# Rows asked for by need, and the opening of a state-space and attention kernel put together anew

## The chip, the cores and the metric

The kernel runs on one core of a Trainium2 chip. The metric is the device time of one execution in microseconds. All data are fp32 apart from two small mask tables in bf16.

## The reference

Two layers, for 8 images of 384 channels and 32 x 32 pixels (1024 tokens). Cut to what matters:

```python
# layer 0, per batch element: a state-space recurrence in both directions, beside a local convolution
xn = x * rsqrt(mean(x*x over channels) + 1e-6) * norm_w
u, z = split(in_proj_w @ xn)                      # 384 channels each
for each direction:                               # tokens forward, tokens backward
    uc    = silu(causal 4-tap depthwise conv of u + conv1d_b)
    dt, Bm, Cm = split(x_proj_w @ uc)             # 24, 16 and 16 rows
    delta = softplus(dt_proj_w @ dt + dt_proj_b)
    h[n]  = exp(delta * A[n]) * h[n] + (delta * uc) * Bm[n]     # 16 states for each channel, along 1024 tokens
    y     = (sum over n of h[n] * Cm[n] + uc * D_param) * silu(z)
g  = out_proj_w @ (y forward + y backward) * scale_mod
lf = sigmoid(3x3 depthwise conv of xn + dw_b) * xn
x  = x + res_scale * (g + lf)
# layer 1, on tokens: causal attention with 6 heads, then a feed-forward block
t  = t + attention(layernorm(t))
t  = t + ffn(layernorm(t))    # sign-binarized weights, activations scaled by their maximum over a group
```

The groups of the feed-forward block's scaling are single batch elements here, and only five of them get anything from it (the reference leaves the rest at zero).

## The kernel before, in words

Channels lie on the 128 partitions in NC = 3 chunks, tokens along the free dimension in two halves of 512. The work consists of three kinds of pieces. Each piece is a list of steps with an estimated time, and the steps of pieces that run together are put in one order by these times. A scheduler then fixes each engine's order: instructions have the priority of the order in which they were emitted, and one that is ready earlier may move ahead. Each engine, and each DMA queue, keeps its order.

`before_scan(b, ...)` (L305) makes what the recurrence of batch b needs. It loads xn, normalizes it, and for each chunk projects it (`in_proj`, L333: four PSUM banks, each of three matmuls, copied out by ACT), runs the 4-tap convolution for two directions and two halves (`conv`, L345: the first tap by ACT, L352, the other three by DVE into PSUM, L362; ACT adds the bias, L363), runs the 3x3 convolution (`local`, L367: nine taps, eight of them on DVE, L383), applies silu and tanh and the residual (`gates`, L417, with a change of ACT's function table before and after), and projects u to the rows of dt, B and C (`project`, L450). Results go to DRAM ("spill"): u in both directions, their sum, silu(z), and the residual with the local part. After the three chunks the rows of B and C are written to DRAM, and twelve `delta` steps (L477) compute delta and delta*u, with four ACT and four DVE instructions each, and store both (L497).

The recurrence is cut in 768 units: a batch, a chunk, one of four parts (direction and half), and two of the 16 states. For a unit the rows of B and of C are read from DRAM and spread over 128 partitions by DMA (tiles bc0 and bc1, 512 KB each). POOL multiplies delta*u by B's rows (L539), ACT computes the decay exp(delta*A) (L552), DVE scans (L557, one scan for each of the two states, in place in the tile g), POOL multiplies by C's rows (L563), and PE adds up over states by transposing g into a PSUM bank (L573). What is done for which unit in slot k stands in `slots` (L1032): the loads of unit k+3, POOL's first product of unit k+2, scans and second product of unit k, the sum of unit k-1. POOL's own order is kept as written. The tile g has 7 buffers, bc0 has 3 and bc1 has 4; they share the SBUF with a pool of 12 `mid` tiles of 1024 elements and 6 `big` tiles of 3072.

`attention` and `feed_forward` of batch b (L621, L905) follow the recurrence of batch b. The first batch's `before_scan` runs alone. Beside the 96 units of its recurrence stand, in this order, the second batch's `before_scan`, `binarize` for w1 and w2 (L194), and the `before_scan` of the third and fourth batch (L1060 to L1066). All later units run beside attention, feed-forward and the other batches' `before_scan` (L1068 to L1090); the last batch's attention comes alone at the end (L1091).

Nearly all loads and stores go through SP's queue (`load`, L109; `spill`, L121; the stores at L254, L472, L497 and L617). SP issues them in its order and stands still at the first one whose tile is not yet free or whose data is not yet made.

Of the kernel before, what the change touches and what calls it, by code (L numbers as in the profile page):

```python
# [9 lines left out]
F32 = mybir.dt.float32  # L10
# [42 lines left out]
def kernel(  # L53
# [19 lines left out]
    const = ctx.enter_context(tc.tile_pool(name="const", bufs=1))  # L73
    small = ctx.enter_context(tc.tile_pool(name="small", bufs=4))
    big = ctx.enter_context(tc.tile_pool(name="big", bufs=6))
    mid = ctx.enter_context(tc.tile_pool(name="mid", bufs=12))
    ptp = ctx.enter_context(tc.tile_pool(name="ptp", bufs=2))
    sp = ctx.enter_context(tc.tile_pool(name="scan", bufs=2))
    dram = ctx.enter_context(tc.tile_pool(name="dram", bufs=5, space=DRAM))
# [114 lines left out]
    def binarize(src, dst, nk, nout, per, name, emit):  # L194

        gs = nout // GROUPS
        st = {}

        def part(w, k, n):
            return w[k * P : (k + n) * P, :].rearrange("(k p) e -> p k e", p=P)  # L200

        def view(k, n):
            t = btile(f"{name}_{k}")
            v = t.rearrange("p c l -> p (c l)")[:, : n * nout].rearrange("p (k e) -> p k e", k=n)
            load(v, part(src, k, n))
            return v

        starts = list(range(0, nk, per))

        @emit  # L210
        def _():
            st["ones"] = small.tile([P, P], F32, name=f"ones_{name}", tag="bones", bufs=1)
            nc.vector.memset(st["ones"], 1.0 / (gs * nk * P))
            st["mps"] = bank(f"mps_{name}", "av")

        for k in starts:

# [15 lines left out]

        @emit
        def _():
            st["mean"] = small.tile([P, GROUPS], F32, name=f"mean_{name}", tag="bmean", bufs=1)
            nc.vector.tensor_copy(st["mean"], st["mps"][:, :GROUPS])

        for k in starts:

            @emit
            def _(k=k, n=min(per, nk - k)):
                v = view(k, n)
                for g in range(GROUPS):
                    z = v[:, :, g * gs : (g + 1) * gs]
                    nc.vector.tensor_scalar(z, z, st["mean"][:, g : g + 1], None, ALU.subtract)
                t = btile(f"sg_{name}_{k}")
                sg = t.rearrange("p c l -> p (c l)")[:, : n * nout].rearrange("p (k e) -> p k e", k=n)
                z, sg = v[:, :, : GROUPS * gs], sg[:, :, : GROUPS * gs]
                nc.scalar.activation(sg, z, AF.Sign)  # L250
                nc.vector.tensor_tensor(sg, sg, z, ALU.subtract)
                nc.vector.tensor_tensor(z, z, sg, ALU.add)
                nc.vector.memset(v[:, :, GROUPS * gs :], 0.0)
                nc.sync.dma_start(out=part(dst, k, n), in_=v)  # L254


    def mean_of(c_of, name):
# [44 lines left out]
                    )  # L302


    def before_scan(b, tags, emit):  # L305

        st = {}
        turns = itertools.cycle(tags)
# [36 lines left out]
        def conv(c, d, h):  # L345

            acc = bank_of(f"u{d}_{b}_{c}_{h}")
            up = st["up", c]
            for s in range(DCONV):
                w = vec[:, c, V_CW + DCONV - 1 - s : V_CW + DCONV - s]  # L350
                if s == 0:
                    nc.scalar.activation(acc, up[:, half(h)], AF.Copy, scale=w)  # L352
                    continue
                lo, hi = h * HB, (h + 1) * HB
                if d == 0:
                    t0, t1 = max(lo, s), hi
                    tap = up[:, t0 - s : t1 - s]
                else:
                    t0, t1 = lo, min(hi, L - s)
                    tap = up[:, t0 + s : t1 + s]  # L360
                to = acc[:, t0 - lo : t1 - lo]
                nc.vector.scalar_tensor_tensor(to, tap, w, to, ALU.mult, ALU.add)  # L362
            nc.scalar.activation(  # L363
                st["u", d, c][:, half(h)], acc, AF.Identity, bias=vec[:, c, V_CB : V_CB + 1]
            )

        def local(c, h):  # L367

            acc = bank_of(f"loc_{b}_{c}_{h}")
            r0, rows = h * (HB // W), HB // W  # L370
            img = acc.rearrange("p (i j) -> p i j", j=W)
            src = st["xn"][:, c, :].rearrange("p (i j) -> p i j", j=W)
            nc.scalar.activation(  # L373
                acc, st["xn"][:, c, half(h)], AF.Copy, scale=vec[:, c, V_DW + 4 : V_DW + 5]
            )
            for k in range(9):
                di, dj = k // 3 - 1, k % 3 - 1
                if k == 4:
                    continue
                i0, i1 = max(r0, -di), min(r0 + rows, H - di)  # L380
                j0, j1 = max(0, -dj), W - max(0, dj)
                to = img[:, i0 - r0 : i1 - r0, j0:j1]
                nc.vector.scalar_tensor_tensor(  # L383
                    to,
                    src[:, i0 + di : i1 + di, j0 + dj : j1 + dj],
                    vec[:, c, V_DW + k : V_DW + k + 1],
                    to,
                    ALU.mult,
                    ALU.add,
                )  # L390
            return acc

        for c in range(NC):

            @emit
            def _(c=c):
                w = mtile(f"win_{b}_{c}", NC * 2 * P).rearrange("p (k i e) -> p k i e", k=NC, i=2)
                for i in range(2):
                    load(
                        w[:, :, i, :],  # L400
                        w_in[:, i * C + c * P : i * C + (c + 1) * P].rearrange("(k p) e -> p k e", p=P),
                    )
                st["win", c] = w
                st["up", c] = mtile(f"up_{b}_{c}")
                st["z", c] = mtile(f"z_{b}_{c}")
                for d in range(2):
                    st["u", d, c] = mtile(f"u{d}_{b}_{c}")

            for i in range(2):
                for h in range(NH):  # L410
                    emit(lambda c=c, i=i, h=h: in_proj(c, i, h), 2.6)
            for d in range(2):
                for h in range(NH):
                    emit(lambda c=c, d=d, h=h: conv(c, d, h), 3.0)


            def gates(c=c):  # L417
                st["xc"] = mtile(f"xc_{b}_{c}")
                load(st["xc"], x[b, chunk(c), :])
                accs = [local(c, h) for h in range(NH)]  # L420
                with tc.high_priority(offset=60):
                    for t in (st["u", 0, c], st["u", 1, c], st["z", c]):
                        pin(nc.scalar.activation(t, t, AF.Silu))
                    for h in range(NH):
                        pin(
                            nc.scalar.activation(
# [12 lines left out]
                usum = mtile(f"us_{b}_{c}")  # L439
                nc.vector.tensor_tensor(usum, st["u", 0, c], st["u", 1, c], ALU.add)  # L440
                spill((b, "us", c), usum, f"sus_{b}_{c}")
                for d in range(2):
                    spill((b, "u", d, c), st["u", d, c], f"su_{d}_{b}_{c}")

            emit(gates, 14.0)


            for h in range(NH):
# [75 lines left out]
    def s_load(u):  # L524
        if u.n == 0:
            for what in ("ud", "dl"):
                t = sp.tile([P, HB], F32, name=f"{what}_{u.name}", tag=what)
                load(t, spilled[u.b, what, u.d, u.c, u.h])
                sst[what, u.b, u.c, u.part] = t
        for i in range(2):  # L530
            r = sp.tile([P, 2, HB], F32, name=f"bc{i}_{u.name}", tag=f"bc{i}", bufs=3 + i)
            rows = spilled[u.b, "rows", u.d][i * NS + u.n : i * NS + u.n + 2, half(u.h)]
            load(r, rows.partition_broadcast(P))
            sst["bc", i, u.name] = r

    def s_first(u):
        g = sp.tile([P, 2, HB], F32, name=f"g_{u.name}", tag="g", bufs=7)
# [494 lines left out]
    def slots(lo, hi):  # L1032
# [2 lines left out]
                f(units[k])  # L1035

        def slot(k):
            at(s_load, k + AHEAD + 1)
            at(s_first, k + AHEAD)
            at(s_scan, k)  # L1040
            at(s_sum, k - 1)
            at(s_gate, k - 1)
# [4 lines left out]
        for f, _ in spread_over(*lists):  # L1047
            f()

    def steps_of(stage, *args):  # L1050
        out = Steps()
        stage(*args, out)
        return out

    per, ahead = len(units) // B, 3
    first = slots(-AHEAD - 1, per + 1)
    others = slots(per + 1, len(units) + 1)
    run(steps_of(before_scan, ORDER[0], ("s", "pt")))  # L1060
    beside = steps_of(before_scan, ORDER[1], ("s", "pt"))
    beside += steps_of(binarize, w1, w1s, NC, FF, 2, "w1")
    beside += steps_of(binarize, w2, w2s, NF, C, 8, "w2")
    for b in ORDER[2 : 1 + ahead]:
        beside += steps_of(before_scan, b, ("s", "pt"))
    run(first, beside)  # L1066

    rest, later, due = [], list(ORDER[1 + ahead :]), [(0.0, 0)]  # L1068
# [74 lines left out]
```

## Time and profile before

| what | value |
|---|---|
| median of 8 runs | 5324.45 us (5308.53 to 5331.47) |
| the profiled execution | 5329.08 us, span 5327.3 us |
| busy, share of the span: PE / DVE / ACT / POOL | 79% / 67% / 51% / 69% |
| granted TensorE clock, mean | 0.861 |
| DMA | 1199.8 MB, 225 GB/s |
| POOL's first product (L539), 768 times | 2381 ns each |
| POOL's second product (L563), 768 times | 2373 ns each |
| load of bc rows, 1536 times | 5.0 us from issue to landing (median) |

A group line of the profile gives the line of the code, the engine, the tiles written and read, their shapes, the count, then the busy time and the mean of one in ns, and after the second bar the idle time of the engine just before these instructions and what ended most of it. A line of the view of waits names the engine and line that waited, what ended the wait, the sum, how many times, and the longest. SPq is SP's queue of DMA issues. A line of the view of stages gives a stretch, its length, then busy time and number of instructions for PE, PEld (weight loads), DVE, ACT and POOL, the granted clock, the DMA engines' busy share and GB/s.

### The profile page before, as it was taken

The numbers are of one execution on the slowest core, as the hardware profiler recorded it, in microseconds if no ns is written. First come the engines' busy times: TensorE is split into PE (matmuls) and PEld (weight loads), VectorE is DVE, ScalarE is ACT, GpSimd is POOL, SyncE is SP. The second block draws the span as 40 slices with busy tenths as digits, with TensorE's granted clock in tenths as the row PEclk, the third lists the DMA queues.
The fourth block names the chain that finished last, engine by engine and source line by source line (L and its number), as shares of the span: only waits on it lengthen the run. The fifth ranks groups of instructions, "written<-read, shape, count | busy, mean of one in ns | idle before, by whom it ended". The sixth has DMA issues, their size and how long they took to land.

```text
span 5327.3 us, 52022 instructions
## 1 busy us (share of the span) xinstructions
PE 4187.0 (79%) x16458; PEld 2200.8 (41%) x16458; DVE 3574.9 (67%) x4243; ACT 2707.3 (51%) x4906; POOL 3672.6 (69%) x1932
## 2 busy tenths in 40 slices
PE   5645566888778889767887788887788888888899
PEld 2222233444334444334444344444344444444444
DVE  7888787666785657765777756677666566666522
ACT  5654554455653645634656445465355354454424
POOL 0666675986768876758876698757687887877700
PEclk7756677989888989888998889898888999999989
DMA  5877777767678667686666876667766767667510
GB/s 188 282 241 261 252 262 270 243 205 239 216 259 272 215 225 240 224 270 219 227 233 229 277 243 219 215 221 236 266 221 214 264 214 239 220 202 228 194 42 24
DMA packets 625116, 1199.82 MB, mean 225 GB/s; under 512 B 44440, under 2 KB 103240, under 8 KB 624840
## 3 DMA queue, kind: packets, MB, share of 16 engines
q1 hardware_dynamic: 621280, 1194.50, 67.7%
q8 instruction: 130, 2.13, 0.2%
q10 hardware_dynamic: 3560, 2.00, 0.1%
q14 instruction: 146, 1.20, 0.1%
HBM read 1030.65 MB, written 165.68 MB: 225 GB/s over the span
## 4 chain that ended last, share of the span: by engine, by line
POOL 32%; issue 23%; DVE 15%; PE 13%; DMA 10%; ACT 5%; SPq 1%; POOLq 0%; ACTq 0%; DVEq 0%
POOL g L539 18%; POOL g L563 14%; DMA bc<-rows 6%; DVE g L557 5%; PE yp L975 2%; PE s L728 2%; DVE loc L383 2%; PE y L573 1%; PE hp L930 1%; DVE u L362 1%; DVE dp L492 1%; PE av L814 1%; PE in L336 1%; DVE du L494 1%; SPq L110 1%
## 5 line engine op out<-in xcount | busy, mean ns | idle before, releaser
L539 POOL TENSOR_TENSOR g<-ud,bc 128x1024 f32<-128x1024 f32 x768 | 1828.4, 2381 | 1038.2 <-DMA bc<-rows 454.9
L563 POOL TENSOR_TENSOR g<-g,bc 128x1024 f32<-128x1024 f32 x768 | 1822.4, 2373 | 251.4 <-issue 120.1
L552 ACT ACTIVATE da<-dl,amat 128x512 f32<-128x512 f32 x1536 | 1057.8, 692 | 1681.6 <-DVE g L557 1608.2
L557 DVE TENSOR_TENSOR_SCAN g<-da,g 128x512 f32<-128x512 f32 x768 | 905.9, 1211 | 609.7 <-POOL g L539 573.3
L573 PE MATMUL y<-ident,g 128*128 128x128 f32 x6144 | 967.4, 305 | 402.6 <-POOL g L563 382.9
L557 DVE TENSOR_TENSOR_SCAN g<-da,carry,g 128x512 f32<-128x512 f32 x768 | 955.6, 1272 | 446.3 <-POOL g L539 428.7
L573 PEld LDWEIGHTS y<-ident,g 128*128 128x128 f32 x6144 | 793.4, 157 | 848.0 <-POOL g L563 533.4
L728 PE MATMUL s<-k,q 64*128 64x512 f32 (+3 forms) x1152 | 452.3, 591 | 175.9 <-ACT pr L749 130.6
L748 DVE TENSOR_REDUCE nm<-s 128x1 f32<-128x512 f32 (+3 forms) x576 | 300.8, 545 | 261.2 <-PE s L737 190.3
L749 ACT ACTIVATE pr<-s,nm 128x512 f32<-128x512 f32 (+3 forms) x576 | 329.1, 574 | 165.3 <-DVE nm L748 153.7
L814 PE MATMUL av<-ptn,v 128*64 128x512 f32 (+3 forms) x1152 | 374.8, 551 | 30.7 <-DVE o L826 26.7
L336 PE MATMUL in<-xn,win 128*128 128x512 f32 x576 | 301.6, 671 | 110.3 <-DMA win<-in_w_in 56.3
L930 PE MATMUL hp<-t,w 128*128 128x512 f32 x720 | 341.7, 621 | 36.5 <-DMA w<-w1s 22.4
L975 PE MATMUL yp<-h,w 128*128 128x512 f32 x720 | 329.3, 615 | 14.6 <-DMA w<-w2s 10.2
L800 PE MATMUL pt<-ident,pr 128*128 128x128 f32 x1728 | 308.0, 303 | 34.5 <-ACT ptn L804 23.3
L804 ACT COPY ptn<-pt 128x512 f32<-128x512 f32 (+3 forms) x576 | 257.6, 479 | 112.4 <-PE pt L800 111.0
L728 PEld LDWEIGHTS s<-k,q 64*128 64x128 f32 x1152 | 159.4, 202 | 338.1 <-ACT pr L749 204.5
L672 PE MATMUL qp<-t,wqk 128*128 128x512 f32 x576 | 268.5, 613 | 11.7 <-DVE t L300 11.6
L800 PEld LDWEIGHTS pt<-ident,pr 128*128 128x128 f32 x1728 | 210.9, 154 | 159.3 <-ACT ptn L804 72.3
L383 DVE SCALAR_TENSOR_TENSOR loc<-xn,vec,loc 128x496 f32<-128x496 f32 (+3 forms) x384 | 254.9, 726 | 9.0 <-ACT loc L373 8.9
L336 PEld LDWEIGHTS in<-xn,win 128*128 128x128 f32 x576 | 119.0, 217 | 253.9 <-issue 151.2
L930 PEld LDWEIGHTS hp<-t,w 128*128 128x128 f32 x720 | 137.2, 199 | 196.9 <-issue 158.9
(151 smaller groups left out, 4623.4 us busy)
## 6 DMA issues: line engine op xcount, KB each, us to landing
bc<-rows SPq DMA_DIRECT2D x1536, 512.0 KB, 5.0
t<-st SPq DMA_DIRECT2D x63, 512.0 KB, 6.1
su<-u SPq DMA_DIRECT2D x48, 512.0 KB, 6.7
du<-su SPq DMA_DIRECT2D x96, 256.0 KB, 5.0
sdl<-du SPq DMA_DIRECT2D x96, 256.0 KB, 2.6
sud<-du SPq DMA_DIRECT2D x96, 256.0 KB, 2.6
ud<-sud SPq DMA_DIRECT2D x96, 256.0 KB, 5.2
dl<-sdl SPq DMA_DIRECT2D x96, 256.0 KB, 5.3
```

What stands on the lines that cost most here:

```text
L336: nc.tensor.matmul(out=mp, lhsT=st["win", c][:, k, i, :], rhs=st["xn"][:, k, half(h)], start=(k == 0), stop=(k == NC - 1),)
L383: nc.vector.scalar_tensor_tensor(to, src[:, i0 + di : i1 + di, j0 + dj : j1 + dj], vec[:, c, V_DW + k : V_DW + k + 1], to, ALU.mult, ALU.add,)
L539: pin(nc.gpsimd.tensor_tensor(g, ud, sst.pop(("bc", 0, u.name)), ALU.mult))
L552: nc.scalar.activation(da, sst["dl", u.b, u.c, u.part], AF.Exp, scale=amat[:, u.c, n : n + 1])
L557: nc.vector.tensor_tensor_scan(gi[:, ::step], da[:, ::step], gi[:, ::step], first, ALU.mult, ALU.add)
L563: pin(nc.gpsimd.tensor_tensor(g, g, sst.pop(("bc", 1, u.name)), ALU.mult))
L573: nc.tensor.matmul(out=y[:, j, :], lhsT=g[:, i, chunk(j)], rhs=ident, is_transpose=True, start=(opens and i == 0 and j == 0), stop=(closes ...
L728: nc.tensor.matmul(out=ss[e][:, : k1 - k0], lhsT=st["q"][rows_of(e), c, chunk(qi)], rhs=st["k"][rows_of(e), c, k0:k1], start=True, stop=(k ...
L800: nc.tensor.transpose(pt[:, chunk(i)], st["pr", c, g, i, e][:, chunk(j)], ident)
L814: nc.tensor.matmul(out=av[rows_of(e), cols], lhsT=st["v"][:, j, hd * HD : (hd + 1) * HD], rhs=st["ptn", j, e][:, cols], start=(j % QT == 0 ...
L930: nc.tensor.matmul(out=hp, lhsT=st["w1"][:, c, chunk(m % 2)], rhs=st["xn"][:, c, half(h)], start=(c == 0), stop=(c == NC - 1),)
L975: nc.tensor.matmul(out=yp, lhsT=st["w2", k // 6][:, k % 6, :], rhs=st["h", k // NC][:, k % NC, half(h)], start=(k == 0), stop=(k == NF - 1),)
```

## The change

1. Rows: in slot k, bc0 is loaded for unit k+4 and bc1 for unit k+2 (both for k+3 before); delta and delta*u for a unit at k+4. bc0 gets a fourth buffer. To make room, the `mid` pool has 11 tiles.
2. 4-tap convolution of the first four batches: with twelve 128x128 diagonal matrices of its weights, made by POOL once into a `big` tile, all four taps become matmuls into the PSUM bank (48 for each batch). ACT's first tap and DVE's three are left out there. The other four batches keep the old form.
3. First batch: 3x3 convolution, silu of z, and the residual (`gates`) move out of its `before_scan` to the head of what stands beside its recurrence. The silus of u and the sum stay (`gates_of_us`), so there are two changes of function table for each chunk more.
4. Weights of `in_proj`: the load for chunk c+1 is emitted at the beginning of chunk c, in every batch.
5. `binarize`: its eight loads and four stores go to ACT's queue.

The diff, cut to its core:

```diff
-    mid = ctx.enter_context(tc.tile_pool(name="mid", bufs=12))
+    mid = ctx.enter_context(tc.tile_pool(name="mid", bufs=11))
...
-            load(v, part(src, k, n))
+            nc.scalar.dma_start(out=v, in_=part(src, k, n))
...
-                nc.sync.dma_start(out=part(dst, k, n), in_=v)
+                nc.scalar.dma_start(out=part(dst, k, n), in_=v)
...
-    def before_scan(b, tags, emit):
+    def before_scan(b, tags, emit, later=None, diags=None):
...
-                if s == 0:
+                if s == 0 and diags is None:
                     nc.scalar.activation(acc, up[:, half(h)], AF.Copy, scale=w)
                     continue
...
-                nc.vector.scalar_tensor_tensor(to, tap, w, to, ALU.mult, ALU.add)
+                if diags is None:
+                    nc.vector.scalar_tensor_tensor(to, tap, w, to, ALU.mult, ALU.add)
+                else:
+                    nc.tensor.matmul(
+                        out=to,
+                        lhsT=diags(c, k),
+                        rhs=tap,
+                        start=(s == 0),
+                        stop=(s == DCONV - 1),
+                        skip_group_check=True,
+                    )
...
+        emit(lambda: weights_of(0))
         for c in range(NC):
...
+                if c + 1 < NC:
+                    weights_of(c + 1)
...
-            emit(gates, 14.0)
+            def gates_of_us(c=c, silus=silus, sum_of_us=sum_of_us):
+                with tc.high_priority(offset=60):
+                    silus([st["u", 0, c], st["u", 1, c]])
+                    pin(nc.scalar.preload_act_table_set(LOG_EXP))
+                sum_of_us()
+
+            if later is None:
+                emit(gates, 14.0)
+            else:
+                emit(gates_of_us, 4.0)
+                later(gates, 10.0)
...
-        for i in range(2):
-            r = sp.tile([P, 2, HB], F32, name=f"bc{i}_{u.name}", tag=f"bc{i}", bufs=3 + i)
-            rows = spilled[u.b, "rows", u.d][i * NS + u.n : i * NS + u.n + 2, half(u.h)]
-            load(r, rows.partition_broadcast(P))
-            sst["bc", i, u.name] = r
+
+    def s_row(u, i):
+
+        r = sp.tile([P, 2, HB], F32, name=f"bc{i}_{u.name}", tag=f"bc{i}", bufs=(4, 4)[i])
+        rows = spilled[u.b, "rows", u.d][i * NS + u.n : i * NS + u.n + 2, half(u.h)]
+        load(r, rows.partition_broadcast(P))
+        sst["bc", i, u.name] = r
...
-            at(s_load, k + AHEAD + 1)
+            at(s_load, k + AHEAD + 2)
+            at(lambda u: s_row(u, 0), k + AHEAD + 2)
+            at(lambda u: s_row(u, 1), k + 2)
...
-    first = slots(-AHEAD - 1, per + 1)
+    first = slots(-AHEAD - 2, per + 1)
...
-    run(steps_of(before_scan, ORDER[0], ("s", "pt")))
-    beside = steps_of(before_scan, ORDER[1], ("s", "pt"))
+
+    taps = btile("taps").rearrange("p c l -> p (c l)")[:, : NC * DCONV * P]
+    taps = taps.rearrange("p (c k q) -> p c k q", c=NC, k=DCONV)
+    for c in range(NC):
+        for k in range(DCONV):
+            nc.gpsimd.tensor_scalar(
+                taps[:, c, k, :], ident, vec[:, c, V_CW + k : V_CW + k + 1], None, ALU.mult
+            )
...
+    beside = Steps()
+    begin = Steps()
+    before_scan(ORDER[0], ("s", "pt"), begin, beside, diags)
+    run(begin)
+    beside += steps_of(before_scan, ORDER[1], ("s", "pt"), diags=diags)
     beside += steps_of(binarize, w1, w1s, NC, FF, 2, "w1")
     beside += steps_of(binarize, w2, w2s, NF, C, 8, "w2")
     for b in ORDER[2 : 1 + ahead]:
-        beside += steps_of(before_scan, b, ("s", "pt"))
+        beside += steps_of(before_scan, b, ("s", "pt"), diags=diags)
```

More of the change, by code (lines that the diff above doesn't have):

```diff
@@ L349, in conv @@
             for s in range(DCONV):
-                w = vec[:, c, V_CW + DCONV - 1 - s : V_CW + DCONV - s]
-                if s == 0:
+                k = V_CW + DCONV - 1 - s
+                w = vec[:, c, k : k + 1]
+                if s == 0 and diags is None:
                     nc.scalar.activation(acc, up[:, half(h)], AF.Copy, scale=w)
@@ L382, in local, with weights_of @@
                 to = img[:, i0 - r0 : i1 - r0, j0:j1]
+                tap = src[:, i0 + di : i1 + di, j0 + dj : j1 + dj]
                 nc.vector.scalar_tensor_tensor(
[L384 to L389, printed above, removed]
-                )
-            return acc
+                    to, tap, vec[:, c, V_DW + k : V_DW + k + 1], to, ALU.mult, ALU.add
+                )
+            return acc
+        def weights_of(c):
+            w = mtile(f"win_{b}_{c}", NC * 2 * P).rearrange("p (k i e) -> p k i e", k=NC, i=2)
+            for i in range(2):
+                load(
+                    w[:, :, i, :],
+                    w_in[:, i * C + c * P : i * C + (c + 1) * P].rearrange("(k p) e -> p k e", p=P),
+                )
+            st["win", c] = w
+        emit(lambda: weights_of(0))
         for c in range(NC):
@@ L396, in _ @@
             def _(c=c):
-                w = mtile(f"win_{b}_{c}", NC * 2 * P).rearrange("p (k i e) -> p k i e", k=NC, i=2)
-                for i in range(2):
[L399 to L403, printed above, removed]
                 st["up", c] = mtile(f"up_{b}_{c}")
@@ L414, in before_scan, with silus, sum_of_us, gates @@
                     emit(lambda c=c, d=d, h=h: conv(c, d, h), 3.0)
-            def gates(c=c):
+            def silus(ts):
+                for t in ts:
+                    pin(nc.scalar.activation(t, t, AF.Silu))
+            def sum_of_us(c=c):
+                usum = mtile(f"us_{b}_{c}")
+                nc.vector.tensor_tensor(usum, st["u", 0, c], st["u", 1, c], ALU.add)
+                spill((b, "us", c), usum, f"sus_{b}_{c}")
+                for d in range(2):
+                    spill((b, "u", d, c), st["u", d, c], f"su_{d}_{b}_{c}")
+            def gates(c=c, silus=silus, sum_of_us=sum_of_us):
                 st["xc"] = mtile(f"xc_{b}_{c}")
@@ L421, in gates @@
                 with tc.high_priority(offset=60):
-                    for t in (st["u", 0, c], st["u", 1, c], st["z", c]):
-                        pin(nc.scalar.activation(t, t, AF.Silu))
+                    us = [st["u", 0, c], st["u", 1, c]] if later is None else []
+                    silus(us + [st["z", c]])
                     for h in range(NH):
@@ L438, in gates @@
                 spill((b, "z", c), st["z", c], f"sz_{b}_{c}")
[L439 to L443, printed above, removed]
-            emit(gates, 14.0)
+                if later is None:
[4 more added lines that the diff above has]
+                    pin(nc.scalar.preload_act_table_set(LOG_EXP))
+                sum_of_us()
+            if later is None:
+                emit(gates, 14.0)
+            else:
+                emit(gates_of_us, 4.0)
+                later(gates, 10.0)
             for h in range(NH):
@@ L529, in s_load @@
                 sst[what, u.b, u.c, u.part] = t
-        for i in range(2):
-            r = sp.tile([P, 2, HB], F32, name=f"bc{i}_{u.name}", tag=f"bc{i}", bufs=3 + i)
-            rows = spilled[u.b, "rows", u.d][i * NS + u.n : i * NS + u.n + 2, half(u.h)]
-            load(r, rows.partition_broadcast(P))
-            sst["bc", i, u.name] = r
+    def s_row(u, i):
[3 more added lines that the diff above has]
+        sst["bc", i, u.name] = r
     def s_first(u):
@@ L1048, in run, with steps_of, diags @@
             f()
-    def steps_of(stage, *args):
+    def steps_of(stage, *args, **kwargs):
         out = Steps()
-        stage(*args, out)
+        stage(*args, out, **kwargs)
         return out
     per, ahead = len(units) // B, 3
-    first = slots(-AHEAD - 1, per + 1)
+    first = slots(-AHEAD - 2, per + 1)
     others = slots(per + 1, len(units) + 1)
-    run(steps_of(before_scan, ORDER[0], ("s", "pt")))
-    beside = steps_of(before_scan, ORDER[1], ("s", "pt"))
+    taps = btile("taps").rearrange("p c l -> p (c l)")[:, : NC * DCONV * P]
[4 more added lines that the diff above has]
+                taps[:, c, k, :], ident, vec[:, c, V_CW + k : V_CW + k + 1], None, ALU.mult
+            )
+    def diags(c, k):
+        return taps[:, c, k - V_CW, :]
+    beside = Steps()
[3 more added lines that the diff above has]
+    beside += steps_of(before_scan, ORDER[1], ("s", "pt"), diags=diags)
     beside += steps_of(binarize, w1, w1s, NC, FF, 2, "w1")
```

## The prediction

> **What bounds the kernel now.** I read the page first, then the busy time of each engine by stage (one stage per batch of the recurrence, cut at the first scan of each batch, every 192nd of L557), then the waits of two stretches.
>
> ```profile
> span 5327.3 us, 52022 instructions
> ...
> PE 4187.0 (79%) x16458; PEld 2200.8 (41%) x16458; DVE 3574.9 (67%) x4243; ACT 2707.3 (51%) x4906; POOL 3672.6 (69%) x1932
> ...
> DVE  7888787666785657765777756677666566666522
> ...
> POOL 0666675986768876758876698757687887877700
> PEclk7756677989888989888998889898888999999989
> ...
> L539 POOL TENSOR_TENSOR g<-ud,bc 128x1024 f32<-128x1024 f32 x768 | 1828.4, 2381 | 1038.2 <-DMA bc<-rows 454.9
> ```
>
> No engine is full over the span. POOL runs two products per unit, 768 x (2.381 + 2.373) = 3651 us, but in the first seven slices DVE has the digits 7 to 8 and POOL 0 to 7, and the granted clock is low. The stages say it in numbers (PE, PEld, DVE, ACT, POOL, clock, DMA):
>
> ```profile
> 139.00:852.00 713.00, 399.76 (x1191) 209.28 (x1190) 596.91 (x696) 386.24 (x577) 465.46 (x239) 0.66 0.78 259
> 852.00:1455.00 603.00, 484.73 (x2003) 257.63 (x2003) 409.19 (x477) 324.65 (x590) 458.78 (x241) 0.90 0.71 232
> ```
>
> The first batch's recurrence takes 713 us against 603 for the second. DVE is at 84% there and PE at 56%; then PE is at 80%, DVE at 68%, POOL at 76%. So the opening is bound by DVE and by what queues behind it, the rest by POOL, PE and DVE in turns. Before it lie 139 us in which POOL runs a single product. The waits of 133 to 930 us, and below them of 930 to 5060 us:
>
> ```profile
> POOL g L539 <- DMA bc<-rows: 180.2, 22, 21.7
> ...
> PE in L336 <- DMA win<-in_w_in: 47.7, 5, 12.7
> ```
> ```profile
> POOL g L539 <- PE y L573: 402.7, 147, 10.3
> POOL g L539 <- DMA bc<-rows: 274.7, 40, 32.4
> ```
>
> POOL waits for rows in both. They take 5.0 us from issue to landing (median), so they are late because SP asks late. In SP's own waits the stores of delta and delta*u stand for 247.2 + 100.6 us behind DVE (L497) and those of gated y for 123.1 us (L617); the rows queue behind them.
>
> ```profile
> SPq L497 <- DVE du L493: 247.2, 90, 9.8
> ...
> SPq L617 <- DVE gy L615: 123.1, 35, 15.8
> ```
>
> **What the Trainium skill says.** "TensorE: Matmul & The Clock Gate", Part 1: the array's clock is gated and released by sustained activity. The stages agree: 0.66 at 56% busy, 0.90 at 80%; work added to an idle PE may therefore be cheaper than at today's clock. "FP8 and Floating Point Precision", TensorE Precision Notes: full fp32 takes 4 passes. The trace shows the price: one 128x512 matmul leaves two records, and L336 has 216 records in 114.8 us of 133 to 930 (1.06 us for each matmul), L975 709 in 324.6 us later (0.92). "DMA: Bandwidth & Descriptors", Issuing engines are not separate DMA queues: another queue saves the issuing time alone. No run shows more yet. So moving w1 and w2 to ACT gives no bandwidth, but takes their waits out of SP.
>
> **The change part by part.**
>
> *Rows.* Before, bc0 and bc1 of unit k+3 are asked for in slot k; bc0 is wanted first, one slot on (L539 of k+3 stands in slot k+1). After, bc0 of k+4 is asked for in slot k (wanted two slots on) and bc1 of k+2 (wanted two slots on instead of three). Nothing is added to any queue. The smaller of the two leads grows by one slot, 4117 us / 663 units = 6.2 us from 930 to 5047. That can't give back 274.7 us: the 40 waits come in some sixteen clusters, around each batch's deltas and the loads of the next attention (L631, L633), and within a cluster SP keeps DVE's pace. I therefore credit a cluster with min(its waits, 6.2): about 80 us. Two thirds of that (POOL, the rows and the issue gaps between them are about that share of the chain from 930) is **-50**. At the bad end bc1 loses a slot: L563 shows no wait for rows today, but eight stops of up to 20.1 us (120.1 in all) that no view explains, and one more of each size is +15. At the good end all the rows' part of the chain would go; it is 5.4% after 930, so -225 is a ceiling, and I keep -120.
>
> *The start, 0 to 139.* Conv taps leave DVE (36 x 0.69 = 25 us) and ACT (12 first taps, 8.2), and the 3x3 convolution with its two finishing steps (31.4 + 4.4 + 4.1 = 40 us DVE) comes after. But PE gets 48 matmuls. A chunk costs PE now 13.2 (in) + 4.6 (xp) us and the three chunks start at 27, 54 and 84, 29 us apart. After: 13.2 + 16 x 1.10 + 4.6 = 35.4 us at today's clock of 0.73, so PE becomes the bound and three chunks end 3 x 35.4 = 106 us after 27, at 133 instead of 118. At 0.92 for each: 3 x (11.0 + 14.7 + 3.8) = 89, ending at 116. PE without gaps should raise the clock, and fetching the weights one chunk early takes away the 4.7 us wait at 54. I take **+5**, range -10 to +16. POOL's 12 products of 128x128 for the taps fall before 27 in its empty slice, at some 0.3 us by its 128x128 operations there (292 ns), 4 us in all.
>
> *The opening, 139 to 852.* Removed from DVE: 108 x 0.692 = 75 us (batches 2 to 4), and 36 first taps from ACT (24.5 us). Added to DVE: 40 us of the first batch's 3x3, less what fits into the start, where DVE loses 65 of 100 us: 0 to 40. DVE goes from 597 to 522-562 us; at today's 84% that is 621 to 669 us instead of 713: -44 to -92. The floor is a later batch, about 600. PE gets 144 x (0.92 to 1.10) = 132 to 158 us, 400 to about 545; of 665 us that is 82%, what the later stages carry. Three more pairs of table loads (1.283 us each, 8 us) go on ACT, which is at 54%. The DMA wait for win (47.7 us) shrinks. With the y transposes queued behind convolutions on PE, I take **-50**, range -95 to +80.
>
> *w1 and w2 on ACT.* 8 loads and 4 stores at about 0.4 us = 5 us of issue. The stores wait for DVE (L254: 22.2 us in two waits on SP); on ACT the decay exponentials (L552) stand behind them, and the scans behind those. **+7**, 0 to +22.
>
> *Buffers.* mid goes from 12 to 11, and the early weights hold one more in every batch: chunks and feed-forward weights meet in four later stages. PE's waits for w1s and w2s are 22.4 + 14.1 us today; win's 4.0 after 930. If both grow fourfold it costs some 110 us of PE waits, half of which I'd see. I take **0** (win lands in 6.8 us in the median, and a chunk's steps are longer), range -5 to +50. The taps take one of six big tiles until the opening's last convolution; hidden by the 3-to-4 that binarizing and one xn need, and if not, binarizing is what slips, used first at 1300.
>
> Sum: -50 + 5 - 50 + 7 + 0 = -88 us. The profiled execution took 5329.1 (span 5327.3), 4.6 above the median of 5324.45. 5329 - 88 = 5241 profiled, **5236** as median. What becomes late next: in the opening PE (y behind conv), later y buffers, POOL's 402.7 us wait for PE.
>
> **The rivals.**
>
> *Rows free the loop.* DVE's delta steps stand behind scans, scans behind POOL, POOL behind rows, rows on SP behind the stores of those deltas. If one slot more breaks that circle, most of the 274.7 us goes, not one slot for each cluster. For it: waits of 2 to 8 us in rows of four or five between 1534 and 1575. Against: DVE is at 77% there and the 20 to 32 us stalls at the attention's loads outlast a slot. -120 instead of -50 and -85 in the opening: about 5140.
>
> *Gains that PE takes back.* Start +16, opening 0, rows -20: within some us of 5320.
>
> *Slower: convolutions on PE's in-order queue.* In the opening PE's idle 313 us is mostly waiting for POOL's products (L573, 275.9 us on weights), which must be followed at once, since POOL has seven g tiles. If the added 158 us doesn't fall into those waits but ahead of transposes, g comes back late, POOL and the scans stop, and the clock stays at 0.66. With share s on the chain the change is -50 (rows) - 68 (DVE's -44 to -92) + 12 + 158 s: it decides from s = 0.67. With s = 1, the start's +16 and the buffers' +50: -50 - 68 + 158 + 16 + 7 + 50 = +113, 5437. For it: PE's clock of 0.50 to 0.66 from 300 to 500. Against: PE idles in long pieces.
>
> That the change doesn't do what it says is the case where the order of issue keeps the rows late anyway: SP's 2346 us behind L563 show that buffers hold it back, but bc0 gets a fourth.
>
> **How the numbers follow.** Forecast case (5190 to 5290): 0.48. Rows free the loop (5130 to 5190): 0.16. PE takes it back (5290 to 5335): 0.16, of which 0.06 within 0.2% (10.6 us, about what a measurement of this kernel can tell from no change) and 0.10 faster. Slower (above): 0.20. Faster 0.74, same 0.06, slower 0.20. Leaving out 0.04 below and 0.13 above gives 5145 to 5360.
>
> **What would show it.** Right: L362 keeps no DVE rows in the first 852 us and PE there has 144 + 48 more matmuls; the first batch's stage is about 660 us with PE near 80% and a clock of 0.8; POOL's wait for rows falls to about 300 of 454.9; the first scan stays within 15 us of 139. Wrong: L573's waits by POOL grow in the opening; L563 waits for rows by over 60 us; PE's waits for w and win grow after 930; da waits behind ACT's stores; or stages after 852 get longer than 600 to 640.

## The result, and the profile after

The changed kernel takes 5257.9 us in the median, 5322.7 before: a ratio of 0.988, 95% interval 0.9867 to 0.9892, some 64 us. The prediction had -88 us with a range from -179 to +36. The size is right, by luck as it turns out: what it is made of is not, and that is what the experiments are about.

Of the page after:

```profile
span 5261.2 us, 53223 instructions
...
PE 4290.2 (82%) x16842; PEld 2252.4 (43%) x16842; DVE 3467.5 (66%) x4105; ACT 2698.8 (51%) x4868; POOL 3678.3 (70%) x1944
...
L572 POOL TENSOR_TENSOR g<-ud,bc 128x1024 f32<-128x1024 f32 x768 | 1828.8, 2381 | 924.4 <-PE y L606 435.4
```

DVE has 107 us less to do, PE 103 us more. POOL's first product (L539 before, L572 now) has waited 114 us less, and what ends most of its waits is no longer the rows but PE. By stages, with the first scans at 161, 833 and 1445 us (PE, PEld, DVE, ACT, POOL, clock, DMA):

```profile
0.00:161.00 161.00, 111.50 (x235) 44.93 (x235) 74.99 (x112) 67.16 (x92) 13.39 (x26) 0.85 0.64 225
161.00:833.00 672.00, 463.89 (x1467) 234.71 (x1466) 515.39 (x600) 381.54 (x555) 459.81 (x237) 0.78 0.77 256
833.00:1445.00 612.00, 489.60 (x2017) 260.76 (x2018) 419.56 (x488) 328.62 (x595) 460.86 (x244) 0.88 0.71 236
```

The start is 22 us longer, the first batch's stage 41 us shorter, so the opening gives 19. The recurrences of the other seven batches, one stretch in each profile, give 48 (the second line is of the changed kernel):

```profile
852.00:5049.00 4197.00, 3447.15 (x14127) 1841.55 (x14128) 2794.56 (x3231) 2146.50 (x3960) 3198.05 (x1679) 0.90 0.71 233
```
```profile
833.00:4982.00 4149.00, 3451.23 (x14130) 1850.80 (x14131) 2799.12 (x3245) 2150.41 (x3961) 3199.25 (x1680) 0.89 0.71 237
```

The same work on PE, DVE, ACT and POOL within 5 us (on the weight loads within 10), in 48 us less. So most of the gain lies where neither taps, nor the moved 3x3, nor binarizing reaches. Of the waits in the whole changed kernel:

```profile
POOL g L572 <- DMA bc<-rows: 313.6, 67, 32.8
...
POOL g L596 <- DMA bc<-rows: 65.2, 25, 14.8
```

The rows of B are waited for 141 us less, those of C, which lost a slot, 65 us.

### The profile page after: what moved, and what is told of

Its sections match the earlier page's. It is cut to its first block, busy times and chain, and to the rows that moved or that the text cites. A ratio compares the mean times of both kernels' runs of the same rounds, so it can differ in the third digit from the quotient of the medians.

```text
span 5261.2 us, 53223 instructions
## 1 busy us (share of the span) xinstructions
PE 4290.2 (82%) x16842; PEld 2252.4 (43%) x16842; DVE 3467.5 (66%) x4105; ACT 2698.8 (51%) x4868; POOL 3678.3 (70%) x1944
## 4 chain that ended last, share of the span: by engine, by line
POOL 32%; issue 22%; DVE 14%; PE 14%; DMA 11%; ACT 5%; SPq 1%; POOLq 0%; ACTq 0%; DVEq 0%
POOL g L572 18%; POOL g L596 13%; DMA bc<-rows 8%; DVE g L590 6%; DVE loc L396 2%; PE yp L1008 2%; PE s L761 2%; PE y L606 1%; DVE dp L523 1%; PE av L847 1%; PE qp L705 1%; PE u L367 1%; PE in L337 1%; PE pt L833 1%; DVE du L525 1%
## 5 line engine op out<-in xcount | busy, mean ns | idle before, releaser
L572 POOL TENSOR_TENSOR g<-ud,bc 128x1024 f32<-128x1024 f32 x768 | 1828.8, 2381 | 924.4 <-PE y L606 435.4
L606 PE MATMUL y<-ident,g 128*128 128x128 f32 x6144 | 936.8, 300 | 284.2 <-POOL g L596 264.0
L606 PEld LDWEIGHTS y<-ident,g 128*128 128x128 f32 x6144 | 777.4, 154 | 698.4 <-POOL g L596 364.6
L337 PE MATMUL in<-xn,win 128*128 128x512 f32 x576 | 279.3, 632 | 41.9 <-ACT up L344 36.8
L1008 PEld LDWEIGHTS yp<-h,w 128*128 128x128 f32 x720 | 138.9, 196 | 174.7 <-issue 171.3
```

Of the source, the lines that this page charges most:

```text
L337: nc.tensor.matmul(out=mp, lhsT=st["win", c][:, k, i, :], rhs=st["xn"][:, k, half(h)], start=(k == 0), stop=(k == NC - 1),)
L572: pin(nc.gpsimd.tensor_tensor(g, ud, sst.pop(("bc", 0, u.name)), ALU.mult))
L606: nc.tensor.matmul(out=y[:, j, :], lhsT=g[:, i, chunk(j)], rhs=ident, is_transpose=True, start=(opens and i == 0 and j == 0), stop=(closes ...
L1008: nc.tensor.matmul(out=yp, lhsT=st["w2", k // 6][:, k % 6, :], rhs=st["h", k // NC][:, k % NC, half(h)], start=(k == 0), stop=(k == NF - 1),)
```

## The experiments

Each kernel below is timed against the kernel before on the same chip, in 5 to 22 executions; two experiments are compared by their ratios. First scans and stages are those of one profiled execution of each. Single executions of one kernel differ by some 20 us and more, so small differences of stages tell nothing by themselves.

**The rows alone** (e1): the kernel before with

```diff
-    mid = ... bufs=12
+    mid = ... bufs=11
-            at(s_load, k + AHEAD + 1)          # with bc0 and bc1, 3 and 4 buffers
+            at(s_load, k + AHEAD + 2)
+            at(lambda u: s_row(u, 0), k + AHEAD + 2)
+            at(lambda u: s_row(u, 1), k + 2)   # 4 buffers each
```

> The kernel before with the rows' part of the change alone: bc0 asked for at k+4 and bc1 at k+2, four buffers each, 11 mid tiles; the opening as before. Theory (the rows carry the part of the gain that lies after the first batch's recurrence, 48 us by the stages of the two profiles): 0.990 to 0.992 of before, about 5275 us, the stages after the first together some 45 us shorter, the first stage some 5 us shorter. Rival (the rows give nothing, since POOL's total wait for rows fell by 76 us only; the later stages gain from the early weights and from a better start of the second batch): 0.998 to 1.000.

Measured: 0.9973 (0.9961 to 0.9985), 14 us. That is far from the theory's 0.990 to 0.992 and clear of nothing, though the interval reaches into the rival's 0.998 to 1.000. POOL's waits in it:

```profile
POOL g L541 <- PE y L575: 431.9, 170, 13.1
POOL g L541 <- DMA bc<-rows: 290.5, 47, 25.7
...
POOL g L565 <- issue: 147.8, 10, 18.4
POOL carry L564 <- DVE g L559: 135.3, 18, 20.4
...
POOL g L565 <- DVE g L559: 93.3, 11, 14.0
POOL g L565 <- DMA bc<-rows: 38.9, 18, 8.9
```

The first product waits 164 us less for rows (454.9 before). Of that, 39 come back as waits for C's rows, 29 as waits for PE (402.7 before), 44 and 19 as waits of the carry and the second product for the scans (91.4 and 74.5), 28 as stops without a named cause (120.1). Those that grew make 159 us, but smaller ones shrank: in all, the idle time before POOL's products and its copies of the carry is 1339 us against 1381, 42 less, as the spans of these two executions differ by 42 us (5285.8 and 5327.3). The two medians differ by about 14. So of the 164 us some 120 were turned into other waits, and of what is left over much is the difference of two single executions. That the next to be late was close behind is how we read this.

**One mid tile less alone** (e2): only the first line of the diff above.

> The kernel before with 11 mid tiles in place of 12, nothing else. Theory (the tile was no loss, as the prediction's zero says): within 0.2% of before, 5312 to 5333 us. Rival (one tile less delays chunks and feed-forward weights): slower by 0.3 to 0.9%, 5340 to 5370 us, PE waiting longer for w1s, w2s and win.

Measured: 1.0009 (0.9991 to 1.0027). The tile costs nothing that can be measured, as the theory said.

**The opening without the rows** (e3): the changed kernel with `s_load`, buffers and mid pool as before.

> The changed kernel with the rows asked for as before (both at k+3, buffers 3 and 4, 12 mid tiles): taps on PE, the first batch's 3x3 beside its recurrence, early weights, w1 and w2 on ACT's queue all stay. Theory: only the opening gains, -41 in the first batch's stage and +22 in the start, so -15 to -25 us against before, 0.995 to 0.997. Rival (the opening's stage gains through the rows, and without them the convolutions on PE cost what they save): 1.000 to 1.006.

Measured: 0.9888 (0.9866 to 0.9909), 60 us. Both lose: it is as fast as the whole change (0.988). The rows add nothing that shows once the rest is there. In its profile the first scan comes at 191 and the second batch's at 835, and the seven later recurrences take 4123 us against 4197 before. Something in this part works after the opening; of its items only the early weights stand in every batch. That its start is 30 us longer than the changed kernel's (191 against 161) costs nothing that shows: the second batch's first scans are 2 us apart (835 and 833).

**Taps of the first batch on ACT and DVE again** (e4): in the changed kernel

```diff
-    before_scan(ORDER[0], ("s", "pt"), begin, beside, diags)
+    before_scan(ORDER[0], ("s", "pt"), begin, beside)
```

> The changed kernel with the first batch's 4-tap convolution on ACT and DVE as before; batches two to four keep it on PE, everything else is as changed. Theory (in the start PE became the bound: 48 matmuls of 0.87 us in 42 us, with DVE half idle): a chunk of the start costs PE 12 + 4.3 us again, the first scan comes at 125 to 140 us instead of 161, and the kernel is 20 to 35 us faster than the changed one, 0.982 to 0.985 of before. Rival (the start is later for other reasons, its loads and the order of the weights; DVE's taps queue behind the 3x3 and binarizing that moved into the start): first scan at 155 to 165, 0.987 to 0.990 of before.

Measured: 0.9865 (0.9842 to 0.9888), first scan at 148 instead of 161, the second batch's at 822 instead of 833. It points the theory's way at less than half its size, and 148 lies between the two expectations' ranges for the first scan; the intervals of the two kernels overlap: not told apart.

**The early weights alone** (e5): the kernel before with

```diff
+        emit(lambda: weights_of(0))
         for c in range(NC):
...
-                (load of win for chunk c)
...
+                if c + 1 < NC:
+                    weights_of(c + 1)
```

> The kernel before with one part of the change alone: the projection's weights for chunk c+1 are asked for at the start of chunk c, in all eight batches. Theory (the stages after the first gained in the run without the rows' part, although nothing of the taps, the 3x3 or binarizing touches them; the early weights are the only part of it that does): 0.991 to 0.994, the gain after the first batch's stage. Rival (PE's wait for these weights was 56 us in all, most of it in the opening, so they matter there or not at all): 0.998 to 1.000 with later stages as before.

Measured: 0.9896 (0.9872 to 0.9919), 55 us of the change's 64. The middle lies beyond even the theory's range (0.991 to 0.994), which the interval just reaches; the rival, that a wait of 56 us can give no more than part of itself in the opening, falls. The recurrences after the first in this run (834 to 4990):

```profile
834.00:4990.00 4156.00, 3430.87 (x14129) 1836.86 (x14129) 2789.58 (x3227) 2153.39 (x3964) 3202.06 (x1680) 0.90 0.71 236
```

4156 us, 41 less than before.

**The opening with all 4-tap convolutions on ACT and DVE** (e6): as e3, with `diags` given to no batch.

> The opening's part of the change without the rows' part, and with the 4-tap convolutions of all batches on ACT and DVE as before; the first batch's 3x3 beside its recurrence, early weights and ACT's queue for w1 and w2 stay. Theory (taps on PE are what shortens the first batch's stage, DVE losing 75 us there, but they lengthen the start): against the same with taps on PE (0.9888) this is slower by 10 to 40 us, 0.991 to 0.996, with a shorter start and a longer first stage. Rival (the taps on PE cost in the start what they give beside the recurrence): 0.986 to 0.990.

Measured: 0.9872 (0.9847 to 0.9898), against 0.9888 with the taps on PE. The theory falls: start and first stage have 110 us less of DVE's work in e3 than here (590 against 700) and 24 us less of ACT's, and that is worth nothing that these runs can tell. The first batch's stage in e3, and in e6 below it:

```profile
191.00:835.00 644.00, 467.47 (x1468) 235.25 (x1468) 488.27 (x560) 365.94 (x529) 454.29 (x236) 0.79 0.76 255
```
```profile
176.00:823.00 647.00, 374.23 (x1180) 199.80 (x1180) 573.97 (x668) 382.53 (x562) 454.39 (x237) 0.69 0.77 257
```

DVE at 76% or at 89%, PE at 73% or at 58%: the stage has the same length, 644 and 647 us. So the relief of DVE bought nothing here. The two kernels move the same work between DVE and PE, though: whether DVE did not set the end, or PE's added work took back what DVE gave, this pair does not tell, and no run takes the work off DVE without giving it to PE.

**w1 and w2 on SP's queue** (e7): as e3, with `load` and `nc.sync` in `binarize`.

> The opening's part of the change without the rows' part, and with the eight loads and four stores of binarizing on SP's queue as before. Theory (12 issues of 0.4 us and two waits of 22 us; the queue matters little): 0.987 to 0.991, the same as with them on ACT's queue. Rival (SP's in-order stores of w1 and w2 hold the rows up, so ACT's queue is part of the gain): 0.992 to 0.997, with POOL's wait for rows in the opening up by 20 us and more.

Measured: 0.9887 (0.9863 to 0.991), as with ACT's queue. The theory holds, and POOL's wait for rows up to 830 us is not longer by 20 us, as the rival had it, but 135.9 us against 172.9 in e3. The first scan comes at 177 here against 191 in e3, and the second batch's at 836 against 835: the queue does move the start, which the part on the start comes back to.

**As e3, with the first batch's taps on ACT and DVE** (e8).

> The opening's part of the change without the rows' part, with the first batch's 4-tap convolution on ACT and DVE and that of batches two to four on PE. Theory (in the start PE is the bound with the taps, 30 us for a chunk against 17 without): first scan some 13 to 30 us earlier than with them, and the fastest version so far, 0.983 to 0.987. Rival (the start's end is set by its loads and by what DVE does beside; what is gained there is lost in the first stage, since start and first stage together were nearly the same in the two profiles with and without the rows' part): 0.988 to 0.990.

Measured: 0.9872 (0.9848 to 0.9895), first scan at 176 against 191. The number lies between the two expectations' ranges, and the interval overlaps e3's: not told apart. With e4 and e6 it says that the choice of engine for the taps moves the first scan by 13 to 15 us, and the whole by nothing that these runs can tell.

**The changed kernel without the early weights** (e9): each chunk asks for its own.

> The changed kernel with one part undone: the projection's weights are asked for at the chunk that uses them; rows, taps on PE, the first batch's 3x3 beside its recurrence and ACT's queue for w1 and w2 stay. Theory (the early weights, 0.9896 alone, are nearly the whole change): 0.997 to 1.003, some 5310 to 5330 us. Rival (the parts overlap, each alone finds the same slack, and without the weights the rest still gives it): 0.988 to 0.992.

Measured: 0.9951 (0.9931 to 0.9971), 26 us. Between the two: the rest of the change gives something, but the greater part of the gain goes with the weights. If the rows make 14 of these 26 us, as in e1, 12 are left for all the rest. In its profile the first batch's recurrence ends at 825 us, 27 earlier than before. That is about what e10 below has with early weights alone (831), and no later than in the changed kernel, which has both (833): in the opening the parts do not add up.

**Early weights for the first four batches** (e10) **and for the last four** (e11), each alone in the kernel before:

```diff
+        early = b in ORDER[:4]        # e11: ORDER[4:]
+        if early:
+            emit(lambda: weights_of(0))
...
+                if not early:
+                    weights_of(c)
+                elif c + 1 < NC:
+                    weights_of(c + 1)
```

> The kernel before with early weights for the first four batches alone (those of the start and of the first batch's stage). Theory (PE's waits for win, 52 of 56 us, lie there, and the first stage got 16 us shorter): 0.996 to 0.998, the first stage 10 to 20 us shorter and the later ones as before. Rival (all of the gain of early weights comes from here, later stages starting in a better order): 0.989 to 0.992.

Measured: 0.9987 (0.9973 to 1.0), 7 us, with an interval that ends at no change at all. The rival falls. In its profile start and first stage end at 831 us instead of 852, as the theory had it, but with one tile less and nothing else (e2) they end at 846, so the median counts.

> The kernel before with early weights for the last four batches alone (those made beside attention and feed-forward). Theory (the stages after the first got 45 us shorter in all with early weights everywhere, above all the third, fifth and sixth, where PE and POOL share the bound, though PE waited 4 us only for win there): 0.990 to 0.994, the first stage as before. Rival (it is the opening that counts): 0.999 to 1.001.

Measured: 0.9919 (0.9887 to 0.9951), 43 us. The place is settled: it is the four batches whose `before_scan` runs beside attention and feed-forward. The cause is not that PE waits less for weights. Its wait for win in the whole run is 59.3 us against 56.3, but most of that lies in the opening, which e11 leaves alone. From the second batch's first scan to the last scan PE waits, in the kernel before and in e11:

```profile
PE hp L930 <- DMA w<-w1s: 22.4, 8, 6.0
...
PE in L336 <- DMA win<-in_w_in: 4.0, 2, 3.0
```
```profile
PE hp L939 <- DMA w<-w1s: 36.5, 13, 6.9
...
PE in L336 <- DMA win<-in_w_in: 3.4, 1, 3.4
```

With the waits for w2s (10.2 and 4.3) that is 36.6 us before and 44.2 in e11, and e11 is 43 us faster. Nor is it the granted clock, in the mean of an execution 0.860 to 0.868 over e11's and 0.858 to 0.870 over those of the kernel before on that chip.

One thing that does differ is PE's order. At the first transpose of each of the 768 units we counted the other instructions that PE had executed. In e11 the count is that of the kernel before at 578 units. The 190 where it is not all lie in units 96 to 671, counted from 0 (the second to the seventh batch), and in that stretch e11 gains what it gains, in several steps of some 6 to 12 us; in the first and the last 96 units the order is the same and nothing is gained. e10 has the order of before from the second batch on (671 of 672 units), and e2 has it at all 768; their seven later recurrences take 4186 and 4193 us, against 4197 before and 4136 in e11. One stretch where the order differs, in PE's timeline (start, length, what, idle time before and what ended it), first before, then e11:

```profile
2201.02 1.07 PE L453 MATMUL xp<-u,wx 128*64 128x512 f32 x2
...
2203.99 10.54 PE L975 MATMUL yp<-h,w 128*128 128x512 f32 x24 [0.31 <-DMA w<-w2s]
...
2215.33 1.93 PE L453 MATMUL xp<-u,wx 128*64 128x512 f32 x6
```
```profile
2194.97 1.93 PE L462 MATMUL xp<-u,wx 128*64 128x512 f32 x6
2200.54 13.27 PE L984 MATMUL yp<-h,w 128*128 128x512 f32 x24 [3.63 <-DMA w<-w2s]
...
2214.61 1.07 PE L462 MATMUL xp<-u,wx 128*64 128x512 f32 x2
```

Of the eight records of a chunk's last projection to dt, B and C (xp), two stand before this group of 24 feed-forward matmuls (yp) in the kernel before and six after it; in e11 it is the other way round. The projection ends behind the same group in both, and over the units around it, whose scans start at 2156 to 2379 us before, e11 gains 7 us. So the stretch shows another order and a small gain, not why the one follows from the other.

Why the order of e11 is the better one is open. For a batch the edit does three things at once: it asks for win earlier; it takes win's `mid` tile a chunk ahead, so that the tiles are handed out in another order and one more is held; and `weights_of(0)` becomes a step of its own, with the default estimate of 2.5 us, which shifts the steps beside it in the common order. No run has one of these without the others.

**Asking early for w1 too** (e12): as e6, and

```diff
-                        st["w1"] = (load of w1 for rows m, m + 1)
+                        st["w1"] = st["w1", m]
+                        if m + 2 < NF:
+                            w1_of(m + 2)
```

> The opening's part of the change with all 4-tap convolutions on ACT and DVE and the rows as before (the run of that gave 0.9872), and in addition the same early asking for the feed-forward's first weights: w1 of rows m+2 is asked for at m. Theory (what win gained is a general gain of asking a chunk ahead; PE waits 22 us for w1s now): 0.981 to 0.985. Rival (asking early helps only where the step that asks is the one that uses; w1's waits are short and a mid tile more is held): 0.986 to 0.990.

Measured: 0.985 (0.9818 to 0.9882). The theory's range, but the interval reaches into the rival's, and e6 has 0.9872. PE's waits for w1s (35.0 us in e6) are no longer among the hundred largest waits. It is the lowest ratio of the study, and not told apart from e4, e6, e8 or the changed kernel.

## Why the prediction was right or wrong, point by point

**Sum and sign: right, by luck.** -88 forecast, -64 measured, in the main case's range (5190 to 5290). But the term priced at -50 for the rows gives 14 alone and nothing that shows beside the rest, and a term priced at nothing gives 55 alone. The two errors largely cancel.

**Buffers and early weights: the step that failed.** The prediction priced the weights at nothing beyond the start and the opening ("I take 0 ... range -5 to +50"), since PE waits 4.0 us for them after 930. Alone they give 55 us, 43 of these in the last four batches. The rule behind the step, that a load fetched earlier is worth the wait that it ends, is what was wrong: in e11 PE waits 3.4 us for win after the opening, 4.0 before, and 43 us are gained. What the runs show in its place is another order of PE's work in the stages that gain; which of the edit's three effects makes it, and why it is faster, stays open. The tile less in the mid pool, the other half of the step, was right at zero.

**Rows: mis-sized.** -50 forecast, -14 alone and nothing measurable on top of the rest. The clusters did shorten, by more than the 80 us credited: from 930 to 5060 us the waits fell from 274.7 to 143.9 in e1, so the lead was not overrated. The factor of two thirds for what lies on the chain was: of 164 us in the whole run some 120 came back as other waits of POOL. A chain counts where POOL's time went, not what would have gone if one of its releasers had come sooner. Even the 14 us need not be the rows' timing alone: in e1 too PE's order differs from that of before, at 117 of the 768 units.

**The start: outside its range.** +22 in the profile against +5 (-10 to +16). The price per matmul was right at its good end, 0.87 us: PE's timeline of the changed kernel has, for the first chunk,

```profile
34.20 11.96 PE L337 MATMUL in<-xn,win 128*128 128x512 f32 x24 [1.49 <-DVE xn L330]
45.99 13.88 PE L367 MATMUL u<-up,taps 128*128 128x512 f32 x32
63.02 4.28 PE L484 MATMUL xp<-u,wx 128*64 128x512 f32 x8 [3.14 <-ACT u L431]
```

12.0 + 13.9 + 4.3 = 30.2 us for a chunk, where 29.5 stood at the good end. The mean clock of 27 to 161 us is 0.83, against 0.66 in the kernel before, as the Trainium skill's "TensorE: Matmul & The Clock Gate", Part 1, made likely. What the step missed is at its two ends. PE's first projection starts at 34.2 instead of 26.6 us, and that comes with w1 and w2 on ACT's queue, a term priced for its issues and stores alone. DVE's order has the sums for binarizing ahead of xn, and they wait for w1's load, so xn comes at 33.4 us; with these loads on SP's queue (e7) it comes at 19.1. DVE's timeline of the changed kernel, then of e7:

```profile
25.80 3.59 DVE L223 TENSOR_REDUCE sums_w<-w 128x1 f32<-128x614 f32 x5 [10.94 <-DMA w<-in_w]
```
```profile
19.05 2.06 DVE L330 SCALAR_TENSOR_TENSOR xn<-xn,vec,ms 128x512 f32<-128x512 f32 x3 [4.27 <-ACT ms L267]
```

From the first projection to the first matmul of the deltas it is 96.3 us, 91.8 before, with waits of 3 us for the silus after two of the three chunks' convolutions. From there to the first scan it is 30.5 us, 20.6 before; what lengthened this last piece was not looked into. Of the 22 us about 8 lie ahead of the first projection, 4 in the chunks and 10 in the deltas. POOL's twelve taps took 602 ns each, not 292.

**The opening: the stage as forecast, the reason not borne out.** 672 us against "about 660", clock 0.78 against 0.8; PE is at 69%, not near 80%. But e3 and e6 have the same length of stage with DVE at 76% and at 89%: what was taken off DVE and given to PE bought nothing that shows. Start and first stage together gave 19 us in the profile, and e10 gets 21 with the early weights alone.

**w1 and w2: +7 forecast, nothing measured.** In range (0.9888 with ACT's queue, 0.9887 with SP's). The path was another, though: not the stores behind DVE, but the loads at the very start, 14 us of the start that the first stage gives back.

**The rivals.** The rows did not free a loop. The slower case did not come: in the changed kernel's first stage (161 to 833) the transposes wait 88.9 us for POOL, 190.0 before (139 to 852), and POOL's wait for PE is 9 us there (161 to 921). PE took the convolutions mostly in its idle time. (The 275.9 us that the prediction sets beside PE's 313 us of idle time are waits of weight loads, and over 133 to 930 us.) Of the marks given, POOL's wait for B's rows at 313.6 (about 300) was met, the first scan within 15 us of 139 was not (161), and the wait for C's rows passed the 60 us named as a bad sign without a loss that shows.

## What to carry to other kernels

Where four engines share the bound in turns, a wait's length says neither what its removal gives nor that removing it is the way to gain: 164 us of one wait gave 14 us, and a load asked for a chunk earlier gave 43 where PE waited 4.0 us for it before and 3.4 after. Change one thing and time it before pricing several by their waits, and price a busy engine's relief only after checking that the stage's length follows it. In a kernel with a static order made by a scheduler, an edit to when a load is asked for can be an edit to the order of all that runs beside it: PE's order changed at 117 of 768 units with the rows and at 190 with the early weights of four batches. Compare the orders in two traces before giving a gain to the edit's own purpose.

## What the runs showed of the hardware

Nothing in the chip's operations was a surprise but one price: a product of 128x128 with a column of scalars on POOL took 602 ns, where its mask instruction and memset of the same shape took 292 and 204.
